# A two-way WKV scan: its decay in a PSUM bank, three matmul tiles instead of four, and one product moved to GpSimd

## The chip, the cores and the metric

The kernel runs on one core of one Trainium2 chip. The metric is the device time of one execution in microseconds; the times before are three such runs. The core's engines work side by side, each through its own instruction queue in order: TensorE (PE in the profile; PEld is its weight load), VectorE (DVE), ScalarE (ACT), GpSimd (POOL) and SyncE (SP, which only starts transfers here). They meet at semaphores. SBUF and PSUM are the two on-chip memories; matmul results land in PSUM[...].

## The reference

Input `x` has the shape (32, 192, 56, 56), float32. Four layers follow each other, each adding its result to its input: an attention with agents, the scan layer, a shift with a small blur, and a long convolution done in the frequency domain. The change touches only the second. Cut to what matters:

```python
def step(carry, kv_t):                       # per channel, over the 3136 pixels of an image
    p, q, o = carry
    kt, vt = kv_t
    no = jnp.maximum(o, u + kt)
    A, Bw = jnp.exp(o - no), jnp.exp(u + kt - no)
    y = (A * p + Bw * vt) / (A * q + Bw)
    no2 = jnp.maximum(w + o, kt)
    A2, B2 = jnp.exp(w + o - no2), jnp.exp(kt - no2)
    return ((A2 * p + B2 * vt, A2 * q + B2, no2), y)
...
k, v, r = xs @ Wk.T, xs @ Wv.T, xs @ Wr.T    # xs: the group-normalized x as tokens
real_w = -jnp.exp(w_decay)
x_bi = 0.5 * (wkv_scan(real_w, u, k, v) + reversed_in_time(wkv_scan)(real_w, u, k, v))
h = jax.nn.sigmoid(r) * x_bi
h = (h - mean(h)) * rsqrt(var(h) + 1e-5) * ln_g + ln_b
x = x + h @ Wo.T
```

`p` is a decayed sum of exp(k)·v, `q` the same of exp(k); `o` only keeps the numbers in range.

## The kernel before

`scan_pairs` does this layer without the running maximum (a guarded version stands ready and runs only if a range check fails; it doesn't run here). It works on two images at once, a *pair*: 2 x 192 channels are laid on three tiles t = 0, 1, 2 of 128 partitions (0 and 1 hold the first 128 channels of each image, 2 the other 64 of both). Each image's 3136 pixels are cut into four *chunks* of 784. There are 16 pairs.

The main loop (L1276 to L1300) runs, for each pair, four *turns*. In one turn the backward scan and the gate are made for a chunk of this pair (`backwards`), normalization, output projection and residual for a chunk that is already through both scans (`finish`), and the forward scan for a chunk of the next pair (`forwards`). Four forward chunks run ahead of the loop, and the last pair has nothing ahead of it, so 60 of the 64 turns hold all three parts. The source order isn't the order on the chip: a scheduler places the instructions of each engine when the program is built, by its own estimate of when each can run, and places the tiles in the buffers. That order is fixed then.

What each part does, per tile t:

- `forwards`: ACT normalizes the loaded `x` (L1110); PE projects it to k and v (L890, L893 for tiles 0 and 1 together; L900, L903 for tile 2) into PSUM tiles; ACT takes exp(k) into `ek` (L1159); DVE multiplies v, still in PSUM, by `ek` into `bv` (L1164). `scan` then runs two recurrences on DVE (L1128), p over `bv` and q over `ek`, each out[i] = decay · out[i-1] + data[i]. The decay is a [128, 1] column of an SBUF tile, spread to 784 columns. After each, DVE adds exp(u) · data to the sums one pixel earlier (L1130). ACT inverts the denominator q by a logarithm and an exponential (L1135, L1136), and DVE multiplies (L1174, into `y`).
- `backwards`: the same scans from the far end over the kept `ek` and `bv`; PE projects r, ACT makes the gate `g` = sigmoid(r) in three steps (L1188, L1192, L1193); DVE forms num · 1/den (L1196), adds it to `y` (L1197) and multiplies by the gate (L1198).
- `finish`: PE centres `y`, ACT squares it (L1213), PE takes the mean of the squares, ACT makes the reciprocal deviation `rd` (L1222, L1223; the third tile's comes by two small DMAs, L1226); PE projects `y` with the output weights; DVE multiplies the result in PSUM by `rd` (L1236) and adds bias and residual (L1239); ACT squares that for the next layer's statistics (L1246).

GpSimd only carries single columns: the value at a chunk's edge into the scan's tile (L1123, an *edge copy*; L1130 needs it) and the last value out of it for the next chunk (L1129), and zeroes for a new pair (L1142).

Every matmul result takes a double PSUM tile, two banks (`turned`, L925): the pool has four of them[...]. A turn uses 17: two for k and two for v of tiles 0 and 1, one each for tile 2, three for r, three for centring, two for the mean, three for the output. A tile can be written again when ACT or DVE has read it.

The tiles `p` and `q` share five SBUF buffers, so a backward scan must wait for an earlier one's sums to be used up.

Of the kernel before, what the change touches and what calls it, by code (L numbers as in the profile page):

```python
# [20 lines left out]
F32 = mybir.dt.float32  # L21
I32 = mybir.dt.int32
AF = mybir.ActivationFunctionType
ALU = mybir.AluOpType
AX = mybir.AxisListType
PSUM = bass.MemoryType.PSUM
# [10 lines left out]
MC = 784  # L37
# [869 lines left out]
def scan_pairs(ctx: ExitStack, tc: tile.TileContext, a, k, x1, st_a, st_c, x2, rs2, count):  # L907
# [5 lines left out]
    nc = tc.nc  # L913
# [2 lines left out]
    kp = ctx.enter_context(tc.tile_pool(name="s_k", bufs=3 * NM))  # L916
    wp = ctx.enter_context(tc.tile_pool(name="s_w", bufs=9))
    sp = ctx.enter_context(tc.tile_pool(name="s_s", bufs=2))
    pp = ctx.enter_context(tc.tile_pool(name="s_p", bufs=4, space=PSUM))
    pairs = _Pairs(nc)  # L920

    def small(name, shape):
        return cp.tile(shape, F32, name=name, tag=name)

    def turned():  # L925
        ps = pp.tile([128, 2, BANK], F32, name="ps", tag="ps")
        return ps, ps[:, :, :HM], [ps[:, h, :HM] for h in range(2)]
# [47 lines left out]
    decay, near, far = small("decay", [128, 2]), small("near", [128, 2]), small("far", [128, 2])  # L975
# [13 lines left out]
    nc.vector.tensor_tensor(near, near, z, ALU.mult)  # L989
    nc.vector.tensor_tensor(decay, near, far, ALU.add)  # L990

    eps = small("eps", [128, 1])
    nc.vector.memset(eps, 4.0 * LN_EPS)
    kept_a, kept_c = small("kept_a", [128, 2, NB // 2]), small("kept_c", [128, NB // 2])
# [5 lines left out]
    def of(t):  # L1000
        return slice(0, 1) if t < 2 else slice(1, 2)
# [105 lines left out]
    def normed(s, m):  # L1107
        xs = load(s.p, m)
        for t in range(3):
            nc.scalar.activation(xs[t], xs[t], AF.Identity, bias=nb1[:, t, s.p : s.p + 1], scale=rs1[:, t, s.p : s.p + 1])  # L1110
        return [parts(t) for t in xs]

    def scan(s, m, t, carry, rev):

        b, e = s.bv[m][t], s.ek[m][t]
        c = eu[:, of(t)]
        got = []
        for i, src in enumerate((b, e)):
            z = wp.tile([128, MC + 1], F32, name="pq"[i], tag="pq", bufs=5)
            edge, last = (MC, 0) if rev else (0, MC)  # L1120
            out, before = (z[:, 0:MC], z[:, 1:]) if rev else (z[:, 1:], z[:, 0:MC])
            at = carry[t][i]
            nc.gpsimd.tensor_copy(z[:, edge : edge + 1], at)  # L1123
            if rev:
                out, data = out[:, ::-1], src[:, ::-1]
            else:
                data = src[:, :]
            nc.vector.tensor_tensor_scan(out, decay[:, of(t)].to_broadcast([128, MC]), data, at, ALU.mult, ALU.add)  # L1128
            nc.gpsimd.tensor_copy(at, z[:, last : last + 1])  # L1129
            nc.vector.scalar_tensor_tensor(before, src, c, before, ALU.mult, ALU.add)  # L1130
            got.append(before)
        return got

    def inverse(s, den, m, t, which):
        nc.scalar.activation(den, den, AF.Ln)  # L1135
        nc.scalar.activation(den, den, AF.Exp, scale=-1.0, accum_out=s.seen[:, which, 3 * m + t : 3 * m + t + 1])  # L1136
# [8 lines left out]
    def forwards(s, m, behind=()):  # L1145
        s.ek[m] = [kp.tile([128, MC], F32, name="ek", tag="ek", bufs=3 * NM + 1) for _ in range(3)]
        s.bv[m] = [kp.tile([128, MC], F32, name="bv", tag="bv") for _ in range(3)]
        s.y[m] = [kp.tile([128, MC], F32, name="y", tag="y", bufs=3 * NM + 4) for _ in range(3)]
        xn = normed(s, m)
        for tiles in ((0, 1), (2,)):  # L1150
            for wt in (wk, wv):
                ps = [turned() for _ in tiles]
                if len(tiles) == 2:
                    pairs.outer(wt, [q[2] for q in ps], xn)
                else:
                    pairs.inner(wt, ps[0][2], xn)
                for t, (_, both, _) in zip(tiles, ps):
                    if wt is wk:
                        nc.scalar.activation(  # L1159
                            s.ek[m][t].rearrange("p (h n) -> p h n", h=2), both, AF.Exp,  # L1160
                            accum_out=s.seen[:, 0, 3 * m + t : 3 * m + t + 1],
                        )
                    else:
                        nc.vector.tensor_tensor(  # L1164
                            s.bv[m][t].rearrange("p (h n) -> p h n", h=2), both,
                            s.ek[m][t].rearrange("p (h n) -> p h n", h=2), ALU.mult,
                        )
                if wt is wk and tiles == (0, 1):
                    for later in behind:
                        later()  # L1170
            for t in tiles:
                num, den = scan(s, m, t, s.fore, False)
                inverse(s, den, m, t, 1)
                nc.vector.tensor_tensor(s.y[m][t], num, den, ALU.mult)  # L1174

    def backwards(s, m):

        xn = normed(s, m)
        h = s.y[m]
        for tiles in ((0, 1), (2,)):  # L1180
            ps = [turned() for _ in tiles]
            if len(tiles) == 2:
                pairs.outer(wr, [q[2] for q in ps], xn)
            else:
                pairs.inner(wr, ps[0][2], xn)
            for t, (_, both, _) in zip(tiles, ps):
                g = wp.tile([128, MC], F32, name="g", tag="t")
                nc.scalar.activation(  # L1188
                    g.rearrange("p (h n) -> p h n", h=2), both, AF.Exp, scale=-1.0,
                    accum_out=s.seen[:, 3, 3 * m + t : 3 * m + t + 1],  # L1190
                )
                nc.scalar.activation(g, g, AF.Ln, bias=1.0)  # L1192
                nc.scalar.activation(g, g, AF.Exp, scale=-1.0)  # L1193
                num, den = scan(s, m, t, s.back, True)
                inverse(s, den, m, t, 2)
                nc.vector.tensor_tensor(num, num, den, ALU.mult)  # L1196
                nc.vector.tensor_tensor(h[t], h[t], num, ALU.add)  # L1197
                nc.vector.tensor_tensor(h[t], h[t], g, ALU.mult)  # L1198
            yield

    def finish(s, m):
# [74 lines left out]
    for p in range(NP):  # L1276
        ahead = State(p + 1) if p + 1 < NP else None
        for i in range(NM):
            m = NM - 1 - i
            back, ending = backwards(s, m), None  # L1280
            if i > 0:
                ending = finish(s, m + 1)
            elif before is not None:
                ending = finish(before, 0)
            next(back)
            if ending is not None:
                next(ending)
            next(back)
            left = next(ending) if ending is not None else []
            if ahead is not None:  # L1290
                forwards(ahead, i, left)
            else:
                for later in left:
                    later()
            if before is not None:
                if i == 1:
                    before.spread = deviations(*moments_of(before), sp, "2")
                elif i == 2:
                    conclude(before)
        before, s = s, ahead  # L1300
# [629 lines left out]
```

## Time and profile before

| | |
|---|---|
| three runs | 12225.82, 12207.08, 12215.15 us (median 12215.15) |
| the profiled execution | 12216.98 us; its span in the profile is 12215.1 us |
| mean granted TensorE clock | 0.958 of full speed |
| busy over the whole span | PE 11030.6 us (90%), DVE 10753.1 (88%), ACT 7146.9 (59%), POOL 3400.5 (28%) |
| loop of `scan_pairs` | 3187.2 us from its first backward scan to its last forward scan; PE busy 2648.1 us, DVE 3099.1, ACT 2029.6, POOL 1877.7 |
| the four forward chunks ahead of the loop | 85.9 us, DVE busy 85.3 |
| from the last forward scan to the stage's end | 153.9 us, DVE busy 131.6 |

The profile is of one execution. Its page gives, among other things, a line per engine with the busy share in 40 equal slices of the span, as a digit in tenths. A group of instructions is shown as: line, engine, operation, output and input tiles with their shape, count, then busy us and mean ns of one, then the time that the engine idled just before them and what ended that. In a timeline each line has start and length in us, and several equal instructions in a row are drawn together (x2 is two).[...] A view of one line's instructions gives least, median and greatest length.

Two such views of GpSimd's lines before: the edge copies L1123 into `p` for the forward scan took 178 ns at least, 1679 in the median and 2737 at most, for one column; the copies L1129 out of `p` 839, 1660 and 3627.

### The profile page before, as it was taken

Reading aid. Unit: us, or ns where it says so; the run is one execution under the profiler, and the core shown is the slowest. Engines: PE = TensorE matmul, PEld = TensorE weight load, DVE = VectorE, ACT = ScalarE, POOL = GpSimd, SP = SyncE. Lnnn points to the kernel's source line nnn. Section 1 sums busy time; section 2 is a strip of 40 time slices with the busy share of each in tenths; the row PEclk is TensorE's granted clock in tenths of the full one; section 3 lists DMA queues with packets and bytes.
Section 4 is the critical chain, followed back from the end, with each engine's and each line's share of the span. In section 5 each row is a group of like instructions: output and inputs, shape, how many; then the busy total and the mean of one; then the engine's idle time right before and its main releaser. Section 6 shows DMA issues by size and latency. Waiting matters only on the chain. (4 is left out here: it accounts for less than half of the span.)

```text
span 12215.1 us, 157485 instructions
## 1 busy us (share of the span) xinstructions
PE 11030.6 (90%) x57358; PEld 6623.6 (54%) x57358; DVE 10753.1 (88%) x14722; ACT 7146.9 (59%) x14690; POOL 3400.5 (28%) x2568
## 2 busy tenths in 40 slices
PE   6999999999999999688888888886999999999999
PEld 3555555555555555333333333333666666666666
DVE  6888888888888888799999999996888899898897
ACT  3555555555555555466666666665666666666665
POOL 0000000000000000455555555555343343343330
PEclk9999999999999999899999999997999999999999
DMA  2222222222222222243334334334333333333331
GB/s 70 57 57 57 59 58 64 59 59 59 63 61 57 57 57 49 73 103 96 97 101 104 93 97 104 98 96 100 71 68 64 67 70 64 67 70 64 67 69 32
DMA packets 1959211, 876.56 MB, mean 72 GB/s; under 512 B 1821153, under 2 KB 1858292, under 8 KB 1949292
## 3 DMA queue, kind: packets, MB, share of 16 engines
q1 hardware_dynamic: 1948188, 840.69, 30.1%
q10 hardware_dynamic: 10240, 25.70, 0.8%
q8 instruction: 458, 7.50, 0.3%
q14 instruction: 325, 2.66, 0.1%
HBM read 482.13 MB, written 319.29 MB: 66 GB/s over the span
## 5 line engine op out<-in xcount | busy, mean ns | idle before, releaser
L619 DVE SCALAR_TENSOR_TENSOR o<-v_a,att_w,o 128x896 f32<-128x896 f32 (+1 forms) x1024 | 1056.8, 1032 | 467.3 <-ACT v_a L593 337.3
L1142 POOL MEMSET f<- 128x1 f32 x96 | 8.9, 99 | 4769.6 <-DMA st_c<-st 4764.6
L1793 ACT COPY y<-ps 64x252 f32<-64x252 f32 (+1 forms) x2376 | 808.7, 340 | 797.3 <-PE ps L1787 767.6
L1626 POOL TENSOR_TENSOR smooth<-smooth,more 114x896 f32<-114x896 f32 x384 | 866.3, 2259 | 1200.7 <-ACT more L1625 1141.2
L1709 PE MATMUL ps<-fixed,real 84*84 84x112 f32 x6144 | 1093.6, 260 | 0.0
L1709 PE MATMUL ps<-fixed,imag 84*84 84x112 f32 x6144 | 1091.1, 259 | 0.0
L1717 ACT ACTIVATE z<-ps,rs 84x112 f32<-84x112 f32 x3072 | 816.7, 355 | 322.1 <-PE ps L1709 319.5
L1709 PEld LDWEIGHTS ps<-fixed,real 84*84 84x84 f32 x6144 | 790.2, 154 | 158.4 <-issue 129.4
L1135 ACT ACTIVATE q<-q 128x784 f32<-128x784 f32 x384 | 328.5, 855 | 812.4 <-DVE q L1130 641.2
L1709 PEld LDWEIGHTS ps<-fixed,imag 84*84 84x84 f32 x6144 | 765.8, 153 | 0.0
L890 PE MATMUL ps<-sq,fixed 128*128 128x392 f32 x512 | 298.9, 746 | 425.9 <-ACT sq L1213 425.9
L636 ACT ACTIVATE pr<-ps,low 98x896 f32<-98x896 f32 (+1 forms) x384 | 352.3, 918 | 559.9 <-DVE low L634 559.9
L724 PE MATMUL ps<-gq_a,xs_a 128*112 128x294 f32 x1792 | 619.1, 427 | 45.7 <-DVE pq L729 45.7
L1787 PE MATMUL ps<-fixed,padded 114*128 114x168 f32 x3072 | 527.6, 322 | 134.6 <-DVE x L1729 118.3
L619 DVE SCALAR_TENSOR_TENSOR o<-v_c,att_w,o 128x448 f32<-128x448 f32 (+1 forms) x1024 | 638.3, 623 | 6.0 <-ACT v_c L604 0.9
L632 PE MATMUL ps<-xs_a,gk_a 128*98 128x448 f32 (+1 forms) x1536 | 637.1, 495 | 0.0
L633 PE MATMUL ps<-xs_c,gk_c 125*98 125x448 f32 (+1 forms) x1536 | 631.6, 492 | 0.0
L1728 PE MATMUL ps<-z,fixed 84*114 84x448 f32 x1536 | 609.7, 539 | 0.4 <-ACT z L1717 0.4
L725 PE MATMUL ps<-gq_c,xs_c 125*112 125x294 f32 x1792 | 608.3, 421 | 0.0
L890 PE MATMUL ps<-x,weights 128*128 128x392 f32 x1536 | 574.0, 517 | 31.1 <-DVE bv L1164 14.2
L737 ACT ACTIVATE pq<-pq 112x1176 f32<-112x1176 f32 x224 | 265.4, 1185 | 553.0 <-DVE pq L729 430.1
L1787 PEld LDWEIGHTS ps<-fixed,padded 114*128 114x128 f32 x3072 | 473.6, 198 | 206.1 <-DVE x L1729 140.5
(372 smaller groups left out, 29249.8 us busy)
## 6 DMA issues: line engine op xcount, KB each, us to landing
x<-x SPq DMA_DIRECT2D x576, 392.0 KB
x<-x SPq DMA_DIRECT2D x512, 196.0 KB
x<-zeros SPq DMA_DIRECT2D x192, 399.0 KB
shifted<-x SPq DMA_DIRECT2D x192, 399.0 KB
x<-x SPq DMA_DIRECT2D x192, 399.0 KB
out_x<-x SPq DMA_DIRECT2D x384, 196.0 KB
x<-in_x SPq DMA_DIRECT2D x32, 1568.0 KB
x<-x SPq DMA_DIRECT2D x32, 1568.0 KB
```

The source lines that it names most:

```text
L619: nc.vector.scalar_tensor_tensor(dst, tap(i), dww[:, t, i : i + 1], dst, ALU.mult, ALU.add)
L632: mm(ps[P2, h, :n], g[:, cols], xs_a[j][:, px], start=True, stop=False)
L633: mm(ps[P2, h, :n], gk_c[0:KC, 2 * j + h, cols], xs_c[j][0:KC, px], start=False, stop=True)
L724: mm(ps[:SUB, i, :HA], xs_a[j][:, px], g, start=True, stop=False)
L725: mm(ps[:SUB, i, :HA], xs_c[j][0:KC, px], gq_c[0:KC, 2 * j + (q + i) // ns], start=False, stop=True)
L890: mm(out, aa, srcs[t][h], start=True, stop=False)
L1626: nc.gpsimd.tensor_tensor(y, y, more, ALU.add)
L1709: nc.tensor.matmul(ps[:84, i * 2 * S : (i + 1) * 2 * S], part[:, i0 + i].rearrange("p s u -> p (s u)"), f3[:, m, :], start=(m == 0), stop= ...
L1717: nc.scalar.activation(z[:, i0 + i].rearrange("p m w -> p (m w)"), ps[:84, i * 2 * S : (i + 1) * 2 * S], AF.Copy, scale=q.rs[:, i0 + i : i ...
L1728: nc.tensor.matmul(got, f4[:, m, :], z[:, i0 : i0 + n, m, :], start=(m == 0), stop=(m == 1))
L1787: nc.tensor.matmul(ps[:, g * 168 : (g + 1) * 168], flat[:, (g0 + g) * 128 : (g0 + g + 1) * 128], f1, start=True, stop=True)
L1793: nc.scalar.copy(y[64 * m : 64 * m + 64, 2 * g0 + i : 2 * (g0 + n) : 2], got[64 * i : 64 * i + 64, :, :, m, :])
```

## The change

```diff
@@ scan_pairs
-    pp = ctx.enter_context(tc.tile_pool(name="s_p", bufs=4, space=PSUM))
+    pp = ctx.enter_context(tc.tile_pool(name="s_p", bufs=3, space=PSUM))
...
     nc.vector.tensor_tensor(decay, near, far, ALU.add)
+    pace = pp.tile([128, 2], F32, name="pace", tag="pace", bufs=1)
+    nc.vector.tensor_copy(pace, decay)
@@ scan
-            nc.vector.tensor_tensor_scan(out, decay[:, of(t)].to_broadcast([128, MC]), data, at, ALU.mult, ALU.add)
+            nc.vector.tensor_tensor_scan(out, pace[:, of(t)].to_broadcast([128, MC]), data, at, ALU.mult, ALU.add)
@@ backwards
-                nc.vector.tensor_tensor(h[t], h[t], g, ALU.mult)
+                nc.gpsimd.tensor_tensor(h[t], h[t], g, ALU.mult)
```

The two decay columns are copied once into a PSUM tile `pace`, and every scan of this stage reads its decay there. To make room for it the pool of double tiles goes from four to three. The gate's product, three a turn, is issued on GpSimd's queue instead of DVE's.

The same arithmetic is done. Since the scheduler places the instructions anew, their order on the engines changes too. In the changed program, in each full turn: DVE begins with the two L1164 of tiles 0 and 1 and then runs each tile's p scan and q scan one after the other, where it began with the two q scans and their L1130 before; ACT runs L1246 of the turn's third tile ahead of the next L1159, where it ran it behind the first two L1159 before; on GpSimd each product stands behind an edge copy. The first tile of v takes the PSUM buffer that the third L1236 reads last, the second one that of the first k tile; the k tiles take those of the first two L1236, where before the first of them took one that L1188 had read. In the turns that also hold the statistics of the pair before, both tiles of r take one and the same buffer in turn.

Lines behind the insertion move by three: L1128 becomes L1131, L1198 becomes L1201, and so on.

## The prediction

> **What bounds the kernel now.** I read the page's forty slices first, then the busy times by stretch, then the instruction groups of the scan stage, then the timeline of one turn of its loop.
>
> ```profile
> span 12215.1 us, 157485 instructions
> ...
> PE   6999999999999999688888888886999999999999
> ...
> DVE  6888888888888888799999999996888899898897
> ...
> POOL 0000000000000000455555555555343343343330
> ```
>
> Slices 17 to 28 are `scan_pairs`, the only stage that the change touches; VectorE (DVE) is at 9 there throughout. The loop's 60 full turns[...] run from the first backward scan at 5082.9 us to the last forward scan at 8270.1:
>
> ```profile
> 5082.90:8270.10 3187.20, 2648.06 (x9659) 1206.42 (x9660) 3099.09 (x3181) 2029.60 (x3486) 1877.72 (x1602) 0.92 0.39 98
> ```
>
> Columns: length, then busy us of PE, PEld, DVE, ACT, POOL. A turn is 3187.2/60 = 53.1 us, of which DVE is busy 3099.1/60 = 51.65 and idle 1.47. Whatever leaves DVE shortens the turn, unless DVE must then wait. Its groups in this stretch:
>
> ```profile
> L1128 DVE TENSOR_TENSOR_SCAN p<-decay,b,bv 128x784 f32<-128x784 f32 x180 | 332.4, 1847 | 0.0
> L1198 DVE TENSOR_TENSOR y<-y,g 128x784 f32<-128x784 f32 x180 | 172.9, 960 | 0.0
> L1236 DVE TENSOR_TENSOR sq<-ps,rd 128x784 f32<-128x784 f32 x177 | 170.3, 970 | 58.7 <-PE ps L893 55.4 <-ACT g L1192 3.2
> L1174 DVE TENSOR_TENSOR y<-p,q 128x784 f32<-128x784 f32 x181 | 169.7, 965 | 0.0
> L1164 DVE TENSOR_TENSOR bv<-ps,ek 128x784 f32<-128x784 f32 x180 | 169.3, 968 | 1.2 <-PE ps L893 1.2
> ```
>
> L1198 is the gate's product, which moves. L1236 holds two thirds of DVE's idle time. The end of one turn and the start of the next, DVE first, then ACT, then PE:
>
> ```profile
> 6543.35 1.03 DVE L1239 SCALAR_TENSOR_TENSOR x<-sq,cb,x 128x784 f32<-128x784 f32 x1
> 6544.31 0.08 DVE L1239 DVE_READ_ACCUMULATOR x<-sq,cb,x 128x1 f32 x1
> 6544.33 3.60 DVE L1128 TENSOR_TENSOR_SCAN q<-decay,f,ek 128x784 f32<-128x784 f32 x2
> 6547.84 1.96 DVE L1130 SCALAR_TENSOR_TENSOR q<-ek,eu,q 128x784 f32<-128x784 f32 x2
> 6549.72 1.85 DVE L1164 TENSOR_TENSOR bv<-ps,ek 128x784 f32<-128x784 f32 x2
> ```
>
> ```profile
> 6543.41 0.80 ACT L1159 ACTIVATE ek<-ps 128x784 f32<-128x784 f32 x1
> ...
> 6545.00 0.94 ACT L1246 ACTIVATE sq<-x,away 128x784 f32<-128x784 f32 x1
> ```
>
> ```profile
> 6542.80 2.90 PE L890 MATMUL ps<-x,weights 128*128 128x392 f32 x8
> 6545.63 1.59 PE L893 MATMUL ps<-x,weights 64*128 64x392 f32 x8
> ```
>
> The reader is to see the cover: `ek` is ready as the last L1239 ends, and DVE spends 5.4 us on the q scans and their L1130, which need only `ek`, while PE finishes the v projection that L1164 reads. Starts also give true costs: a scan takes 1.755 us from start to start (two from 6544.33 to 6547.84), L1130 0.94, a product 0.89.
>
> [...] in the last stage:
>
> ```profile
> 9425.25 4.87 POOL L1626 TENSOR_TENSOR smooth<-smooth,more 114x896 f32<-114x896 f32 x2 [45.38 <-ACT more L1625]
> ```
>
> ```profile
> 9426.19 1.07 DVE L1664 TENSOR_REDUCE sums<-sq 114x16 f32<-114x896 f32 x1
> 9427.18 0.98 DVE L1696 TENSOR_TENSOR imag<-a,a 84x420 f32<-84x420 f32 x1
> 9428.09 0.67 DVE L1690 TENSOR_TENSOR a<-re,g 84x504 f32<-84x504 f32 x1
> ```
>
> L1696 (two SBUF inputs) takes 0.98 instead of its least 0.58; the reduction and L1690 (a PSUM and an SBUF input) are not stretched.[...] I expect no faster scan.
>
> **Part by part, per turn.** *Gate product off DVE:* three L1198 at 0.89 = -2.67. DVE's work becomes 48.98.
>
> *Decay in PSUM:* twelve scans. The nearest rows, L1164 (a PSUM input) at 968 ns and L1174 (SBUF only) at 965, price PSUM at nothing.[...] I take 0. The one copy into `pace` is nothing.
>
> *The product on GpSimd:* L1626's fastest, 2.068 us for 896 elements, scaled to 784: 1.81 us. GpSimd is busy 1877.7 of 3187 us, much of it tiny copies[...] (0.18 us free, up to 2.7 behind DVE), so 180 x 1.81 = 326 us fit. In the changed program's instruction order, each product stands behind one edge copy (0.2). Product 0 falls on two scans (3.5 us): nothing. Product 1 falls on two L1236 (PSUM and SBUF, 1.77 us) and ends about 0.3 into the L1239 behind them. Product 2 falls on one L1236 and holds the last L1239 back by 0.2 + 1.81 - 0.8 = about 1.25. Sum +1.55; bounds 0[...] and 3 x 1.81. What queues behind the products, edge copies of the next forward scans, has some 5 us to spare before its L1130.
>
> *Three double tiles instead of four:* the k projection used to take a tile that ACT freed early; now both of its tiles are those that two L1236 free, and the v projection gets the third L1236's tile and the one that `ek` frees. The build reacts with another order, and this I hold to be the decisive part. DVE now runs L1164 twice first and then p and q scans; and ACT has the square of the last L1239 (L1246) ahead of `ek` instead of behind it. So at each turn's end a chain lies open: L1239 starts; +1.07 ACT begins L1246 (as 6541.39 to 6542.46 in the trace); +0.95 `ek`; +0.90 its tile is free; PE's second half of the v projection, two L890 at 0.36 and eight L893 in 1.52; +0.05. L1164 starts 5.25 us after L1239 instead of 0.98: a stall of +4.25. What covered this were the q scans, which now stand behind it. Bounds: 0.5, if `ek` were not held by L1246[...].
>
> Behind L1164 DVE's whole turn is queued, and ACT's L1135 and PE's next tiles with it. No DMA changes its queue; SP's loads only trade places within a turn.
>
> *What goes:* the wait of L1236 for PE (about 1.0). In the new order ACT's third L1213 comes some 28 us after L1164 (DVE's operations up to the q scan's L1130 that ACT waits for ahead of it, plus ACT's own); PE then needs 1.5 + 3.0 + 4.4 us for the rest of the mean, one receptance tile and the output projection, to 37 us, and DVE is at L1236 after 41. About 0.2 of other waits stays.
>
> Sum: 48.98 + 4.25 + 1.55 + 0.2 = 54.98 against 53.1, +1.86; times 60 = +112 us. The four forward chunks ahead of the loop and the four backward ones behind are about even. The profiled execution took 12216.98 us (span 12215.1), 0.02% from the median 12215.15: 12216.98 + 112 = **about 12,325 us**.
>
> **Rivals.** *Faster: the wait is not there.* If ACT and PE get ahead far enough that L1164 finds its tile, as in the trace of before, where it waits 1.2 us in all, DVE keeps its 1.47 idle: -2.67 x 60 = -160, **12,057 us**; half of it, 12,137. For it: DVE is the bound, PE has 17% to spare. Against: L1164 reads `ek`, and `ek` stands behind the last L1239 in ACT's queue. *No change:* the chain is as I say, but the products collide with nothing: 1.86 - 1.55 = +0.3 a turn, **12,235 us**. For it: GpSimd's copies stretch no scan now (least 1817 ns, most 1861), so DVE may always win. Against: L1696 above. *Slower still: PSUM is not free* for the scan[...]; or[...] products 0 and 1 too delay DVE by up to 1.81: +3.3 x 60, about 12,520. Against: L1690's row.[...]
>
> **Chances.** Likeliest case 0.48 (own range 12,255 to 12,390, from both unknown costs); faster 0.25; no change 0.12; slower still 0.15. 0.2% (24 us) is about what a measurement of this kernel can tell from no change. Faster 0.25, same 0.12, slower 0.63. Range 12,130 to 12,410[...].
>
> **What would show it.** Right: DVE's busy time in the stage falls by about 170 us, but idle time before L1164 rises to some 4 us a turn, put down to PE or `ek`; the last L1239 of a turn lasts 2 us or more; tiny GpSimd copies fall to 0.2 us beside scans; scans stay near 1.84. Wrong: L1164 waits under 2 us a turn, or the scans' mean moves by over 50 ns.

## The result and the profile after

| | before | after |
|---|---|---|
| median | 12214.14 us (4 runs, 12207.08 to 12225.82) | 12346.53 us (4 runs, 12338.17 to 12351.77) |
| profiled execution | 12216.98 us, span 12215.1 | 12351.77 us, span 12349.8 |
| loop of `scan_pairs` | 3187.2 us | 3318.8 us |

The changed kernel is slower: ratio 1.0107, 95% interval 1.0092 to 1.0122. The page's head and three of its forty-slice rows:

```profile
span 12349.8 us, 157627 instructions
...
PE   7999999999999999688888888887899999999999
...
DVE  6888888888888888798998989996888888898897
...
POOL 0000000000000000244444444444433433343330
```

In the slices 18 to 27, where DVE stood at 9 before (the stage's first and last slice, 17 and 28, had 7 and 6, so the prediction's "throughout" is too much), eights have come in. POOL has fallen from 5 to 4 although it got more work. The loop by busy time (columns as before: length, then PE, PEld, DVE, ACT, POOL):

```profile
5094.80:8413.60 3318.80, 2754.51 (x9663) 1224.30 (x9662) 3000.73 (x3000) 2045.39 (x3484) 1395.31 (x1780) 0.96 0.38 94
```

A turn is 3318.8/60 = 55.31 us, of which DVE is busy 50.01 and idle 5.30. Before it was 53.12, 51.65 and 1.47. So 1.64 us of DVE's work went and 3.83 of waiting came. DVE's groups in this stretch, and GpSimd's:

```profile
L1131 DVE TENSOR_TENSOR_SCAN p<-pace,b,bv 128x784 f32<-128x784 f32 x180 | 331.6, 1842 | 0.0
...
L1242 DVE SCALAR_TENSOR_TENSOR x<-sq,cb,x 128x784 f32<-128x784 f32 x177 | 235.7, 1332 | 2.1
...
L1177 DVE TENSOR_TENSOR y<-p,q 128x784 f32<-128x784 f32 x179 | 171.6, 958 | 3.0 <-ACT q L1139 3.0
L1167 DVE TENSOR_TENSOR bv<-ps,ek 128x784 f32<-128x784 f32 x180 | 169.5, 969 | 295.3 <-PE ps L893 295.3
L1239 DVE TENSOR_TENSOR sq<-ps,rd 128x784 f32<-128x784 f32 x177 | 165.9, 964 | 0.0
```

```profile
L1201 POOL TENSOR_TENSOR y<-y,g 128x784 f32<-128x784 f32 x180 | 356.4, 1980 | 76.9 <-DVE y L1200 57.6 <-DVE away L1246 14.9
...
L1132 POOL COPY f<-p 128x1 f32<-128x1 f32 x180 | 34.2, 190 | 876.2 <-DVE p L1131 876.2
```

The wait of 58.7 us before `sq<-ps,rd` is gone, and 295.3 us stand before `bv<-ps,ek`, 4.92 a turn. The x update L1242 (L1239 before) grew from a mean of 1031 ns to 1332, 53 us in all. The scan is what it was (1842 against 1847 ns), but the one-column copy behind a p scan now takes 190 ns in the mean and 183 in the median, where its median was 1660.

One end of a turn, engine by engine: DVE, ACT, PE.

```profile
6503.10 1.85 DVE L1242 SCALAR_TENSOR_TENSOR x<-sq,cb,x 128x784 f32<-128x784 f32 x1
...
6510.28 1.86 DVE L1167 TENSOR_TENSOR bv<-ps,ek 128x784 f32<-128x784 f32 x2 [5.13 <-PE ps L893]
6512.05 1.84 DVE L1131 TENSOR_TENSOR_SCAN p<-pace,f,bv 128x784 f32<-128x784 f32 x1
```

```profile
6505.18 0.95 ACT L1249 ACTIVATE sq<-x,away 128x784 f32<-128x784 f32 x1 [0.99 <-DVE away L1246]
...
6506.13 0.80 ACT L1162 ACTIVATE ek<-ps 128x784 f32<-128x784 f32 x1
```

```profile
6503.11 1.58 PE L890 MATMUL ps<-x,weights 128*128 128x392 f32 x4
6507.07 1.58 PE L890 MATMUL ps<-x,weights 128*128 128x392 f32 x4 [2.38 <-ACT ek L1162]
6508.59 1.59 PE L893 MATMUL ps<-x,weights 64*128 64x392 f32 x8
```

Read from the bottom up: `bv` waits for L893; its second half could only begin at 6507.07, when ACT had read the k tile into `ek`; ACT began that at 6506.13 because the square of the last x update stood ahead of it; and that update ran from 6503.10 for 1.85 us instead of 1.03. The four recorded L890 ahead of this gap are the first v tile's, whose buffer the third `sq<-ps,rd` had freed.

The rest of the program adds up to little. The four forward chunks ahead of the loop took 97.8 us instead of 85.9, with 12.3 us of the same wait before `bv`; the end of the stage took 152.4 instead of 153.9, and everything behind it 7 us less. With the loop's +131.6 that makes the +134.7 of the span.

### The profile page after: what moved, and what is told of

Read it like the earlier page. It is cut to its first block, busy times and chain, and to the rows that moved or that the text cites. A ratio compares the mean times of both kernels' runs of the same rounds, so it can differ in the third digit from the quotient of the medians.

```text
span 12349.8 us, 157627 instructions
## 1 busy us (share of the span) xinstructions
PE 11142.0 (90%) x57358; PEld 6643.6 (54%) x57358; DVE 10640.8 (86%) x14531; ACT 7157.0 (58%) x14690; POOL 2895.0 (23%) x2760
## 5 line engine op out<-in xcount | busy, mean ns | idle before, releaser
L619 DVE SCALAR_TENSOR_TENSOR o<-v_a,att_w,o 128x896 f32<-128x896 f32 (+1 forms) x1024 | 1056.0, 1031 | 469.8 <-ACT v_a L593 340.1
L890 PE MATMUL ps<-x,weights 128*128 128x392 f32 x1536 | 627.3, 541 | 305.4 <-ACT ek L1162 130.1
L890 PEld LDWEIGHTS ps<-x,weights 128*128 128x128 f32 x1536 | 278.0, 198 | 624.3 <-DVE sq L1239 190.3
```

Of the source, the lines that this page charges most:

```text
L619: nc.vector.scalar_tensor_tensor(dst, tap(i), dww[:, t, i : i + 1], dst, ALU.mult, ALU.add)
L890: mm(out, aa, srcs[t][h], start=True, stop=False)
```

## The experiments

Each run is compared with the kernel before, timed beside it on the same chip. The runs fall into three groups on three chips, beside which the kernel before took 12223.78, 12219.92 and 12227.91 us (12214.14 in the result); a difference between runs of two groups is uncertain by about as much as these differ. Line numbers shift with the edits; tile names don't. Groups of instructions are shown for the stretch from 5095 to 8300 us, which holds 59 or all 60 of the full turns. The theories named in the expectations: A is the prediction's (the new order lays a chain open at the end of the turn, and the products collide a little), B says that three tiles are too few in any order, C that the product on GpSimd is itself the cost.

### The product alone on GpSimd

The kernel before, with the last line of the diff only.

```diff
-                nc.vector.tensor_tensor(h[t], h[t], g, ALU.mult)
+                nc.gpsimd.tensor_tensor(h[t], h[t], g, ALU.mult)
```

> Only the gate's product moves to GpSimd; four double tiles, the decay in SBUF. DVE begins the turn with the two q scans again, but ACT has all three squares (L1246) ahead of the k exponential. Theory A (the loss of the change is the chain at the turn's end that the new instruction order lays open[...]):[...] the three products cost 3 to 4 us and save 2.67; the first q scan waits about 2 us for ek behind the last square. About 12,400 us (12,330 to 12,420), L1128 idle some 2 us a turn. Theory B (three tiles are too few, whatever the order): with four tiles nothing stalls, some 12,060 to 12,280. Theory C (the product on GpSimd is what costs): about 12,345, as the whole change.

Measured: 12259.75 us, ratio 1.003 (1.0018 to 1.0041). That is in theory B's range and well below A's 12,330, but B's mechanism, that nothing stalls with four tiles, isn't what the trace shows. Two of DVE's groups:

```profile
L1128 DVE TENSOR_TENSOR_SCAN q<-decay,b,ek 128x784 f32<-128x784 f32 x180 | 418.0, 2322 | 0.0
...
L1128 DVE TENSOR_TENSOR_SCAN q<-decay,f,ek 128x784 f32<-128x784 f32 x177 | 321.9, 1846 | 80.4 <-ACT ek L1159 80.4
```

With the decay in SBUF, one backward q scan in three nearly doubles (up to 3449 ns; mean 2322 instead of 1836, 1.46 us a turn), and a new wait for `ek` of 80.4/59 = 1.36 us a turn has come. Together they are more than the 2.67 us that the product took off DVE. The collision is real, but A had put it at 3 to 4 us a turn: over the loop DVE's busy time fell by 0.48 us a turn, so 2.2 of the 2.67 came back.

### The decay in PSUM and three tiles, product on VectorE

The changed kernel with that last line undone.

> The decay in PSUM and three double tiles; the gate's product stays on DVE. DVE begins the turn with L1167 (v times ek) ahead of the scans, but ACT has the k exponential ahead of the last square, unlike the whole change. Theory A: L1167 still waits for the second half of the v projection, which starts when ek has freed its tile, but no longer for the square: idle 2 to 3 us a turn instead of 4.9, DVE's work 51.65 us as before; about 12,295 us (12,260 to 12,340). Theory B: the stall of 4.9 us stays, about 12,440. Theory C: no product on GpSimd, no loss, 12,215.

Measured: 12319.06 us, ratio 1.0074 (1.0057 to 1.0091), in A's range. The wait before `bv` is 161.3 us in the stretch, 2.75 a turn, and the x update is back at 1031 ns. So most of the loss is there without any product on GpSimd. This doesn't yet part the order from the number of tiles.

### Three tiles alone

The kernel before with one number changed.

```diff
-    pp = ctx.enter_context(tc.tile_pool(name="s_p", bufs=4, space=PSUM))
+    pp = ctx.enter_context(tc.tile_pool(name="s_p", bufs=3, space=PSUM))
```

> The kernel before with one change: three double PSUM tiles in turn instead of four; decay in SBUF, gate's product on VectorE. VectorE keeps the old order here (the two q scans ahead of the v products bv) and ScalarE has the last square behind two of the three k exponentials. Theory A (the loss came from the order, which left a chain open, not from the number of tiles): 12,220 us (12,195 to 12,260), the wait before bv under 0.5 us a turn. Theory B (three tiles are too few whatever the order): 12,300 us or more, with the wait before bv at 2 us a turn or above.

Measured: 12300.3 us, ratio 1.0067 (1.005 to 1.0084). Here theory A missed: DVE kept the old order, the wait before `bv` was 0.8 us in all, and the time still rose by 80 us. The time is B's, its place isn't. Two DVE groups, then PE at one turn's end:

```profile
L1128 DVE TENSOR_TENSOR_SCAN q<-decay,f,ek 128x784 f32<-128x784 f32 x177 | 320.8, 1840 | 61.9 <-ACT ek L1159 61.9
...
L1196 DVE TENSOR_TENSOR p<-p,q 128x784 f32<-128x784 f32 x177 | 171.5, 969 | 86.5 <-ACT q L1136 86.5
```

```profile
6511.00 1.58 PE L890 MATMUL ps<-x,weights 128*128 128x392 f32 x4 [0.84 <-DVE sq L1236]
6514.96 0.92 PE L893 MATMUL ps<-x,weights 64*128 64x392 f32 x2 [2.38 <-ACT x L1110]
6516.09 2.98 PE L890 MATMUL ps<-x,weights 128*128 128x392 f32 x4 [0.21 <-DVE sq L1236]
```

The k projection now waits for tiles that L1236 frees, and longer for the normalized `x`; so `ek` comes after DVE is done and the first q scan waits. Over the loop the k, v and r projections of tiles 0 and 1 (L890, L893) waited 37.1 us for L1236 and 119.0 for L1110; before, none is listed for L1236 and 8.2 for L1110. The runs don't part the two. In the kernel before, DVE waited 10.2 us before the q scan, 13.6 before L1196 and 58.7 before L1236. The last is gone here too: it has mostly moved to L1196 (88.1 over the loop), and the wait before the q scan (63.2) is the new one. Over the loop DVE idles 2.6 us a turn instead of 1.47.

### The square behind the exponentials

The changed kernel with one order fixed on ScalarE: the square of the third tile's x update stands behind the two `ek`, where the kernel before had it. The dependency only orders two instructions of one engine. By the two traces DVE and GpSimd run the whole loop in the same order as in the changed kernel, and ScalarE's order differs by this square alone.

```diff
-                        nc.scalar.activation(
+                        grown = nc.scalar.activation(
                             s.ek[m][t].rearrange("p (h n) -> p h n", h=2), both, AF.Exp,
...
-                    for later in behind:
+                    for later in behind[:-1]:
                         later()
+                    for later in behind[-1:]:
+                        squared = later()
+                        link = mybir.DependencyInfo(mybir.DependencyClass.NoSync, mybir.DependencyReason.DATA)
+                        tc.add_manual_dep(squared.ins, grown.ins.name, link, reason="ek first")
```

> The whole change with one order pinned: the third square L1249 may not run on ACT ahead of the two k exponentials. Nothing else is asked for. Theory A: the k exponential starts when its matmuls and ACT's work in hand are done, about 3 us earlier; the wait of L1167 falls from 4.9 us a turn to about 2; about 12,165 us (12,130 to 12,220). Theory B: the tile, not ACT's order, is what is late: within 40 us of 12,346. Theory C: within 40 us of 12,346.

Measured: 12190.43 us, ratio 0.9972 (0.9961 to 0.9983). That is in A's range. Moving one activation of 0.95 us turns a loss of 132 us into a gain of 33.

```profile
L1246 DVE SCALAR_TENSOR_TENSOR x<-sq,cb,x 128x784 f32<-128x784 f32 x180 | 239.1, 1328 | 2.1
...
L1167 DVE TENSOR_TENSOR bv<-ps,ek 128x784 f32<-128x784 f32 x180 | 169.6, 970 | 131.9 <-PE ps L893 131.9
```

The x update (here L1246) is as long as in the changed kernel, but the wait before `bv` fell from 4.92 to 2.2 us a turn. One end of a turn, DVE and ACT:

```profile
6528.73 1.91 DVE L1246 SCALAR_TENSOR_TENSOR x<-sq,cb,x 128x784 f32<-128x784 f32 x1
...
6533.27 1.86 DVE L1167 TENSOR_TENSOR bv<-ps,ek 128x784 f32<-128x784 f32 x2 [2.62 <-PE ps L893]
```

```profile
6528.84 0.80 ACT L1162 ACTIVATE ek<-ps 128x784 f32<-128x784 f32 x1
...
6530.68 0.95 ACT L1253 ACTIVATE sq<-x,away 128x784 f32<-128x784 f32 x1
```

`ek` starts 0.11 us after the x update here, and 3.03 after it in the changed kernel. So this order alone makes more than half of the stall, with three tiles and three products on GpSimd left in place. What is left of it is the rest of the chain, from `ek` over the freed tile to the second half of the v projection.

### The third product back on VectorE

```diff
-                nc.gpsimd.tensor_tensor(h[t], h[t], g, ALU.mult)
+                (nc.vector if t == 2 else nc.gpsimd).tensor_tensor(h[t], h[t], g, ALU.mult)
```

> The changed kernel with one edit: the gate's product of the third tile stays on VectorE (two of three products on GpSimd); the order of the rest is the same. Theory A (the third product runs into the last x update, which it holds back by 0.9 us, as much as VectorE's own product costs): no gain from having moved it, 12,346 us (12,320 to 12,365), the last x update of a turn back at 1.03 us, the wait before bv unchanged at 4.9 us a turn. Rival (the long x update has another cause than the product): 12,400 us (12,380 to 12,420), since VectorE gets 0.89 us a turn more work and the x update stays at 1.9.

Measured: 12189.41 us, ratio 0.997 (0.9957 to 0.9982). Neither theory had that, and the expectation was wrong that the order of the rest stays. With the product on DVE the scheduler puts the square behind `ek` by itself; why isn't shown (presumably it now reckons the last x update later). ScalarE at one turn's end:

```profile
6485.99 0.80 ACT L1162 ACTIVATE ek<-ps 128x784 f32<-128x784 f32 x1
...
6486.78 0.81 ACT L1162 ACTIVATE ek<-ps 128x784 f32<-128x784 f32 x1
...
6487.72 0.95 ACT L1249 ACTIVATE sq<-x,away 128x784 f32<-128x784 f32 x1
```

DVE's groups:

```profile
L1242 DVE SCALAR_TENSOR_TENSOR x<-sq,cb,x 128x784 f32<-128x784 f32 x180 | 187.0, 1039 | 0.0
...
L1167 DVE TENSOR_TENSOR bv<-ps,ek 128x784 f32<-128x784 f32 x180 | 169.1, 967 | 135.3 <-PE ps L893 132.6 <-ACT x L1113 2.7
```

It is thus to be compared with the run before it, which has that order too: 12190.43 with three products on GpSimd, 12189.41 with two. The third product saves DVE 0.89 us and lengthens the x update by about as much (1328 ns in the mean against 1039, 0.87 us a turn). The changed kernel's timelines show it, GpSimd first, then DVE:

```profile
6557.75 1.85 POOL L1201 TENSOR_TENSOR y<-y,g 128x784 f32<-128x784 f32 x1 [1.00 <-DVE y L1200]
```

```profile
6558.53 1.91 DVE L1242 SCALAR_TENSOR_TENSOR x<-sq,cb,x 128x784 f32<-128x784 f32 x1
```

The update is under way for a microsecond when the product ends (6559.60), and takes 0.84 more, nearly its whole own time.

### The q recurrence first

To the version with the square behind `ek`, the order of the two recurrences is turned round in the source (p first before), so that the scheduler prefers the one that needs only `ek`.

```diff
-        for i, src in enumerate((b, e)):
+        for i, src in ((1, e), (0, b)):
...
-            got.append(before)
+            got.insert(0, before)
```

> As the one before, and the source has the q recurrence ahead of the p one, after which DVE begins the turn with one q scan and its L1133 (2.7 us, both need only ek) ahead of L1167. Theory A: these 2.7 us cover what is left of the wait: under 1 us a turn before L1167, about 12,060 us (12,030 to 12,120). Theory B and C: over 12,250.

Measured: 12120.64 us, ratio 0.9913 (0.9897 to 0.993), 0.6 us above A's range and faster than both kernels. In the loop the wait before `bv` is 40.0 us, and 75.1 stand before the q scans.

### The v products tied behind the q sums

The same, with the forward q scans of both tiles of a pair issued ahead of the v projection, and the next `bv` ordered behind the last q sum (`one` is the body of `scan` for one recurrence).

```diff
+                if wt is wk:
+                    dens = {t: one(s, m, t, s.fore, False, 1) for t in tiles}
...
+                        tc.add_manual_dep(made.ins, summed[-1].ins.name, link, reason="q first")
```

> The fastest version so far (12,120 us) with the v products bv tied behind the q sums on VectorE, and the q scans of both tiles of a pair first, as in the kernel before. Theory A (what is left of the stall, 0.7 us a turn before bv, is order): 12,080 us (12,040 to 12,105), the wait before bv under 0.1 us a turn; what stays is the wait of the first q scan for ek, some 1.2 us a turn. Rival (VectorE must wait for PE in one place or the other): 12,105 to 12,145 us, the wait only changes its place.

Measured: 12113.9 us, ratio 0.9914 (0.9897 to 0.993); the interval of the last run, so no difference between them is shown. In the loop the wait before `bv` is gone (0.0) and the one before the q scans is down to 29.8 us, but the wait before `sq<-ps,rd`, which the change had removed, is back with 58.2. The waiting mostly changed its place, as the rival had it.

### The decay back in SBUF, twice

Each of the last two versions with the scan reading `decay` again; three tiles, and the bank stays reserved.

```diff
-            nc.vector.tensor_tensor_scan(out, pace[:, of(t)].to_broadcast([128, MC]), data, at, ALU.mult, ALU.add)
+            nc.vector.tensor_tensor_scan(out, decay[:, of(t)].to_broadcast([128, MC]), data, at, ALU.mult, ALU.add)
```

> The fastest version so far (12,120 us: the changed kernel with the last square behind the k exponentials and the q recurrence first) with one change: the scans read the decay from SBUF again; the bank of its own stays, unused by them. Theory D (the decay in PSUM is what lets GpSimd's product run beside scans): backward scans that lie beside a product grow to some 2.3 us as in the run with the product alone on GpSimd, +1.4 us a turn, 12,205 us (12,160 to 12,260). Rival (the bank does nothing[...]): 12,095 to 12,145 us, scans at 1.84 us.

> The version with the v products tied behind the q sums (12,114 us), with the scans reading the decay from SBUF again. Theory D[...]: the third to fifth parts of a turn's products stretch VectorE by some 2 us a turn as in the other run with the decay in SBUF, and later x updates make PE late: 12,290 us (12,230 to 12,330). Rival (the +190 us of that run came from the order that the planner made[...]): 12,100 to 12,180 us.

("Third to fifth parts" is a slip; the turn's three products are meant.) Measured: 12311.41 us, ratio 1.0077 (1.006 to 1.0094), which is 191 above its partner, twice what was expected; and 12298.93 us, ratio 1.0059 (1.0042 to 1.0075), 185 above. (Taken against the kernel before of each group, the two differences are 195 and 177.) GpSimd, then DVE, in the first of them:

```profile
6503.21 3.40 POOL L1205 TENSOR_TENSOR y<-y,g 128x784 f32<-128x784 f32 x1
```

```profile
6503.12 1.84 DVE L1131 TENSOR_TENSOR_SCAN q<-decay,b,ek 128x784 f32<-128x784 f32 x1
6504.89 2.55 DVE L1204 TENSOR_TENSOR y<-y,p 128x784 f32<-128x784 f32 x1
```

The product, issued 0.09 us after the scan, takes 3.40: it ends 1.65 us after the scan, nearly a whole product later, and DVE's next operation, 2.55 long, ends 0.83 after the product. Read so, the product waited for the scan, and DVE's next operation for the product. The changed kernel's counterpart, product and scan:

```profile
6489.48 1.87 POOL L1201 TENSOR_TENSOR y<-y,g 128x784 f32<-128x784 f32 x1
```

```profile
6489.31 1.84 DVE L1131 TENSOR_TENSOR_SCAN p<-pace,b,bv 128x784 f32<-128x784 f32 x1
6491.08 1.82 DVE L1131 TENSOR_TENSOR_SCAN q<-pace,b,ek 128x784 f32<-128x784 f32 x1
```

Side by side, neither is stretched. That this is no matter of order is seen from all scans of a program. One group from the first pair, without and with the decay in SBUF (least, median, greatest length in ns):

```profile
L1131 DVE TENSOR_TENSOR_SCAN q<-pace,b,ek x192: 1817/1841/1872, 5085.1 to 8278.2; 128x784 f32<-128x784 f32 x192
L1131 DVE TENSOR_TENSOR_SCAN q<-decay,b,ek x192: 1819/1839/3426, 5079.1 to 8441.5; 128x784 f32<-128x784 f32 x192
```

In the six programs with the decay in PSUM no scan is longer than 1.877 us; in the four with it in SBUF and products on GpSimd the longest take 3.43 to 3.46; in the two with it in SBUF and every product on DVE, 1.86. So in these programs a scan is stretched where both come together, its decay column in SBUF and a product on GpSimd. Its start value, another column in SBUF that every version reads, doesn't do it alone (1.877 us at most with the decay in PSUM). Over the loops (first backward to last forward scan) the first pair stands at 3261.5 and 3097.2 us, with DVE busy 3124.5 and 2969.1: nearly all of that loss is DVE's stretched operations. In the second pair it is 3258.9 and 3083.7, busy 3077.7 and 2972.7: some 105 us stretched, 70 more of waiting. The built order changed in both pairs too (in the first, DVE now begins a turn with two q scans ahead of `bv` instead of one), so not all of the 185 to 191 us is shown to come from the collision: what the stretched operations show directly is 155 and 105 us.

### The product and ScalarE's order, four tiles

The kernel before with the product on GpSimd and the square behind `ek`, decay in SBUF.

> The kernel before with two changes: the gate's product on GpSimd, and the last square tied behind the two k exponentials on ScalarE; four double tiles and decay in SBUF as before. The product alone gave 12,260 us, with 1.5 us a turn of waiting for ek. Theory A (that wait is ScalarE's order): 12,170 us (12,135 to 12,205), the wait before the first q scan under 0.4 us a turn, backward scans still stretched to 2.3 us. Theory C (the product itself is what costs): 12,240 to 12,275 us, the same as the product alone.

Measured: 12213.8 us, ratio 0.9997 (0.9988 to 1.0006), between the two. The wait for `ek` fell from 80.4 to 50.3 us only, and one backward q scan in three is still stretched (mean 2321 ns). So the product on GpSimd without the bank gains nothing here, with ScalarE's order mended or not.

## Why the prediction was right, and where it was off

- *Product off DVE, scan time in PSUM, L1236's wait:* as forecast. That the decay in PSUM would cost a scan nothing and make it no faster was an estimate from the rows of other operations; the scans' means are 1826 to 1846 ns (1835 to 1847 before), and the wait for PE is 0.0.
- *The stall before `bv`:* the order that the prediction held to be decisive is shown by the fixed square to be more than half of it. The term was mis-sized: 4.92 us a turn instead of 4.25. The chain from the last x update to `bv` was put at 5.25 us; the timeline has 7.18. Of the difference 0.8 is PE's second half, counted as "two L890 at 0.36": it is four, 1.52 us from start to start, as the prediction's own line of eight for two tiles shows. Another 0.8 is the lengthened x update, which the collision term holds. In this turn ACT also waits for the small L1246. The lower bound of 0.5, "if `ek` were not held by L1246", was too low: in the run with just that, 2.2 us a turn are left.
- *Collisions:* 53/60 = 0.89 us a turn instead of 1.55. Product 0 costs the two scans beside it nothing (1.84 and 1.82 us in the timeline), as forecast; the author's estimate for this rested on L1696 and L1690 alone. The product took 1.86 in the median (1.81 forecast), but product 1 costs the first x update only 0.06 instead of 0.3 (1.09 in the timeline), and product 2 holds the last one back by 0.85 instead of 1.25: the update starts 1.0 us behind L1239 and not 0.8, and ends 0.84 after the product, about 0.2 less than its own 1.03.
- *The sum:* 50.01 + 5.30 = 55.31 us a turn against 54.98 forecast; the errors of the stall (+0.67) and of the collisions (-0.66) cancel, which is luck. The 0.33 that is left is 0.18 of other waits (0.38 instead of 0.2; 0.2 alone is a wait for the square in the statistics, 12.7 us before L1093) and 0.14 of other busy time on DVE. The forward chunks ahead of the loop weren't "about even": they have the same open chain, +12 us. The median came out 21 us above the forecast.
- *What would show it:* DVE's busy time fell by 98 us and not by "about 170". A collision lengthens records (the x update's mean from 1031 to 1332 ns) and so counts as busy, which that line forgot. The last x update of a turn lasts 1.85 to 1.91 us, not the "2 us or more".
- *"This I hold to be the decisive part" (the order):* right for this program, too narrow as a reason. Three tiles cost 80 us with DVE's old order at the turn's end too, mostly by a later `ek` (53 of the loop's 70 us). Yet a loss needn't be: with two orders mended, the same three tiles, bank and products take 12,121 us.

The rival "the wait is not there" failed: the wait is there, even with the square behind `ek`, and its 12,057 us wasn't reached by any run. That the products collide with nothing is excluded by the x update's records (1.85 and 1.91 us beside a product, 1.03 before).

## What to carry to other kernels

When work leaves the bounding engine, look at what has covered the next transfer or matmul there, and compare the built order of every engine at the seam, not only of the engine that was relieved: one 0.95 us activation ahead of the wrong neighbour cost some 160 us here (12,347 against 12,190). An operand of two columns decided here whether GpSimd's product and a DVE operation beside it were stretched (3.40 and 2.55 us with the decay in SBUF; with it in PSUM the product took 1.87 beside scans of 1.84 and 1.82), so price the pair (decay's place and product's place) together: with three tiles, the product on GpSimd and the decay in SBUF took 12,299 and 12,311 us, no less than three tiles alone (12,300). What the product's move is worth in the fastest version isn't known: no run has the mended orders with the bank and every product on DVE, and none the mended orders in the kernel before. Of several operations to be moved, the one that runs beside a short chain of operations that must wait for it may gain nothing: the third product didn't (the x update took 1328 ns with it and 1039 without, the program 12,190 us and 12,189).

## What the runs showed of the hardware

The size was unexpected: at the same scan length in the median (1.84 us), one operand column in SBUF instead of PSUM, with the order that the scheduler makes of it, moves the whole program by 185 to 191 us. Even one-column copies of GpSimd show it: behind a forward p scan, a mean of 185 ns with the column in PSUM and 1670 without (first pair). And the collision cost both sides, one after the other: in the pair of records above the product is longer by 1.5 us (3.40 against 1.87), and then DVE's next operation by 1.6 (2.55 against 0.96). In the profile that counts as busy time, not as idle.
